# Three-layer EdgeConv graph network on one core: the next row's first edge by a product, and rows of A at a pitch of 512 elements

## The chip, the cores and the metric

The kernel runs on one core of one Trainium2 chip. The metric is the device time of one execution in microseconds. Three runs of the kernel before gave 522.43, 522.38 and 520.69 us, so its median is 522.38 us.

## What is computed

There are 2500 nodes with 256 features and 80,000 edges, sorted by destination. The reference normalizes x by rows, applies a ReLU, sends the result through three EdgeConv layers that average over each node's incoming edges, and multiplies all four feature matrices by a final weight.

```python
def _edge_conv(x, src, dst, W, b):
    xi = x[dst]
    xj = x[src]
    m = jnp.concatenate([xi, xj - xi], axis=-1) @ W + b
    s = jax.ops.segment_sum(m, dst, num_segments=N)
    cnt = jax.ops.segment_sum(jnp.ones((dst.shape[0],), m.dtype), dst, num_segments=N)
    return s / jnp.maximum(cnt, 1.0)[:, None]
...
h = jnp.maximum(_layernorm(x, axis=-1), 0.0)
for W, b in ((W0, b0), (W1, b1), (W2, b2)):
    h = jax.nn.relu(_edge_conv(h, src, dst, W, b))
    xs.append(h)
x = x + jnp.concatenate(xs, axis=-1) @ Wf + bf
```

## The kernel before

The kernel turns the sum over edges into a product with a matrix of counts: A[i, j] is how often node i is the source of an edge to node j. A layer is then the product of z = h times the lower half of the weight with A, plus a product of h with the difference of the weight's halves, weighted by the node's count. z is split into a high part zh and a low part zl, both in the 32-bit format fp32r, so each product with A is made twice.

The 2500 destination nodes are cut into 417 windows of 6, and the windows into five groups, four of 84 windows (504 columns of A) and one of 81 (486 columns). The part of A for one group is a tile `a` of 128 partitions by NT = 20 rows (of source nodes) by G = 504 columns (`new_a`, line 733). Two such tiles live in two pools, `apool0` and `apool1`, which take turns. A group's tile is built in the first layer (`build`, `counts`, `take_counts`: comparisons on VectorE, small products on TensorE, a copy by ScalarE), stored to DRAM (`finish`, line 788) and loaded again in the layers after (`load_a`, line 794), except for the two groups whose tiles are still held.

`layer` (line 802) makes one group of one layer: for each of the 20 rows and each of the two halves o it multiplies zh and zl with the row `a[:, i, :n]` (line 817), 80 products in all. Eight products with the weight `wt` follow or are mixed in (line 821), and ScalarE takes the result. Three layers of five groups make 1200 products with A. In the first layer they run through an order-keeping wrapper, so that the profile gives them the wrapper's line 280. In the layers after, they stand at line 817. `nodes_split` (line 692) makes the next z, with the bias row `brow` for the last tile of nodes, and `final` (line 715) the product with the final weight.

Before A can be built, the kernel must find where each window's edges begin. The destinations are laid out as 128 rows of 625 (`dst_i`). `find_first` (line 494) takes the first entry of each row as `first`, and the first entry of the row after it as `after`; that second one comes from a separate load, `next_i`, of 127 single numbers with a stride of a row (line 408). `find_rows` (line 499) compares both with the windows' limits `limr`, which gives `behind` and the selection `pick`. `pick_half` multiplies `pick` with the destinations, `count_half` counts on ScalarE, `search` makes the edges' offsets, and `get_edges` gathers them by GpSimd's indirect DMAs.

The order of work in this first part, the head, is written out by hand as a string of names (line 849) that `perform` runs through: each name issues its instructions on its engine, and each engine keeps that order. The names that matter here are `warm22` (22 products with a tile of zeros, made ahead of the next product that asks for it: `keep_warm`, `warmed`), `lim` and `io` (small constants), `dstr` (destinations to fp32r on ScalarE), `st0 rs0 sq0 sc0 N0` (statistics, square root on ScalarE, scales, and normalization of the first two tiles of x), `first`, `pick`, `pk00` and so on (`pick_half`), `sg` (`count_half`), `se` (`search`), `ge` (`get_edges`), `T`, `R` (transposes and their copies), `Z` (product with the layer's weight `wb`) and `F` (product with the final weight `wf`).

The loads at the start stand in the order of SP's queue: x tiles 0 and 1, `next_i`, x tiles 2 to 5, `wb`, x tiles 12 to 19, `wf`, `wt`, then three bias rows into `brow`. ScalarE's queue has the destinations and x tiles 6 to 11.

Tiles are laid out one after another in the order of their pools and names: `const`, `wpool` (weights), `hot` (comparisons), then `apool0` and `pre` or `apool1`. In the kernel before, `a` begins at byte 148,320 of a partition in `apool0` and at 188,640 in `apool1`. Both are 96 modulo 128. A row of A has 504 elements of 4 bytes, 2016 bytes, so that rows 0, 1, 2, 3 of four begin at 96, 64, 32 and 0 modulo 128, and so on around.

Of the kernel before, what the change touches and what calls it, by code (L numbers as in the profile page):

```python
# [8 lines left out]
F32 = mybir.dt.float32  # L9
I32 = mybir.dt.int32  # L10
AF = mybir.ActivationFunctionType
OP = mybir.AluOpType
# [4 lines left out]
def general(ctx: ExitStack, tc: tile.TileContext, x, src, dst, Ws, bs, Wf, bf, out):  # L17
# [12 lines left out]
    EB = J * P  # L30
    G = 512
    NG = NP // G
    TG = G // P
    KL = 5
    CELLS = NP * NP
    BIG = 4096.0
    assert E == NCH * P and NCH == NB * J and NP % G == 0 and NT % KL == 0 and EB < BIG
    assert CELLS + EB < 2 ** 24
# [84 lines left out]
    def count_block(b):  # L123
        row = ps_big.tile([P, 2, G], F32, name="big").rearrange("p a n -> p (a n)")
        for j in range(J):
# [73 lines left out]
    def group(l, g):  # L199
        hl, hn = h[l % 2], h[(l + 1) % 2]  # L200
        pa = ps_big.tile([P, 2, G], F32, name="big")
        if l == 0:
# [39 lines left out]
    for l in range(L):  # L242
        for g in range(NG):
            group(l, g)
# [21 lines left out]
F32R = mybir.dt.float32r  # L266
# [20 lines left out]
def run(it):  # L287
    for _ in it:
        pass
# [16 lines left out]
def chain(*its):  # L306
    for it in its:
        yield from it
# [3 lines left out]
def by_windows(ctx: ExitStack, tc: tile.TileContext, x, src, dst, Ws, bs, Wf, bf, out, missing):  # L312
    nc = tc.nc
    PE, DVE, ACT, POOL, SP = nc.tensor, nc.vector, nc.scalar, nc.gpsimd, nc.sync
    PEo, DVEo, POOLo, ACTo, SPo = (InOrder(tc, e) for e in (PE, DVE, POOL, ACT, SP))
    P = 128
    N, D = x.shape
    E = src.shape[0]
    NT = (N + P - 1) // P
    NP = NT * P  # L320
    LAST = N - (NT - 1) * P
    L = len(Ws)
# [13 lines left out]
    while sum(GWS) < NW:  # L336
        GWS.append(min(84, NW - sum(GWS)))
    G = max(GWS) * W
    NG = len(GWS)
    Q = NT // 2  # L340
    assert NT == 2 * Q
    PAD = 96
# [7 lines left out]
    const = ctx.enter_context(tc.tile_pool(name="const", bufs=1))  # L350
# [9 lines left out]
    def bank():  # L360
        return ps[-1].tile([P, 512], F32, name="bank")
# [8 lines left out]
    away = const.tile([P, WG, CAP], BF16, name="away")  # L370
    cnt = const.tile([P, NP], BF16, name="cnt")
    share = const.tile([P, NT], F32, name="share")
    brow = const.tile([P, L, D], F32, name="brow")
    bf_sb = const.tile([P, D], F32, name="bf_sb")
    ident = const.tile([P, P], F32, name="ident")
    ones = const.tile([P, 1], F32, name="ones")
    ones_b = const.tile([1, 1], BF16, name="ones_b")
    ident_b = const.tile([P, P], BF16, name="ident_b")
# [4 lines left out]
    nc_ = const.tile([P, W + 2], F32, name="nc_")  # L383
    deg_b = const.tile([P, WG, W], BF16, name="deg_b")
    lim = const.tile([P, WG], F32, name="lim")
    a_dram = [dram.tile([P, NT, G], F32, name=f"a_dram{g}") for g in range(NG)]

    apools = [ctx.enter_context(tc.tile_pool(name="apool0", bufs=1))]
    pre = ctx.enter_context(ExitStack())
    pp = pre.enter_context(tc.tile_pool(name="pre", bufs=1))  # L390
    pw = pre.enter_context(tc.tile_pool(name="prework", bufs=2))


    dst_rows = dst.rearrange("(p c) -> p c", p=P)
# [5 lines left out]
    def load_x(queue, a, b):  # L400
        queue.dma_start(acc[:, a:min(b, NT - 1), :], xr[:, a:min(b, NT - 1), :])
        if b == NT:
            queue.dma_start(acc[:LAST, NT - 1, :], x[(NT - 1) * P:N, :])

    chunks = [(0, 2), (2, 6), (6, 12), (12, NT)]
    load_x(SPo, *chunks[0])
    next_i = pp.tile([P, 1], I32, name="next_i")
    SPo.dma_start(next_i[:P - 1], dst_rows[1:P, 0:1])
    load_x(SPo, *chunks[1])
    load_x(ACTo, *chunks[2])  # L410
    ws = [None] * L
# [2 lines left out]
    def load_wb(l, queue=SP):  # L414
        ws[l] = wpool.tile([P, DC, D], F32, name="wt"), wpool.tile([P, DC, D], F32, name="wb", bufs=1)
        queue.dma_start(ws[l][1], Ws[l][D:2 * D, :].rearrange("(c p) d -> p c d", p=P))

    def load_wt(l, queue=SP):
        queue.dma_start(ws[l][0], Ws[l][0:D, :].rearrange("(c p) d -> p c d", p=P))
# [14 lines left out]
    row_i = pp.tile([P, MORE], I32, name="row_i")  # L434
    POOLo.iota(row_i, pattern=[[0, MORE]], base=-P, channel_multiplier=1)
    make_identity(nc, ident)
    im_i = pp.tile([P, NT * S], I32, name="im_i")
    POOL.iota(im_i, pattern=[[1, NT * S]], base=0, channel_multiplier=0)
    POOL.memset(brow, 0.0)
    nc_i = pp.tile([P, W + 2], I32, name="nc_i")  # L440
    POOL.iota(nc_i, pattern=[[-1, W + 2]], base=1, channel_multiplier=0)
    for l in range(L):
        SP.dma_start(brow[PAD:PAD + 1, l, :], bs[l].rearrange("(o d) -> o d", o=1))
    DVE.memset(ones, 1.0)
    DVE.memset(ones_b, 1.0)
    DVE.memset(cnt[:, NV:], 0.0)
# [12 lines left out]
    def warmed(to):  # L459
        for _ in range(cold[0]):  # L460
            PEo.matmul(to, idle[:, :P], idle, start=True, stop=True)
        cold[0] = 0
        return to
# [5 lines left out]
    first = pp.tile([P, 1], F32, name="first")  # L469
    after = pp.tile([P, 1], F32, name="after")  # L470
    behind = pp.tile([P, WG * P], F32, name="behind")
    pick = pp.tile([P, WG * P], F32R, name="pick")
# [14 lines left out]
    def limits():  # L487
        DVEo.tensor_copy(lim, lim_i)
        DVEo.tensor_copy(limr, limr_i)
        DVEo.tensor_scalar(unlim, lim, -1.0, 0.5, op0=OP.mult, op1=OP.add)  # L490
        DVEo.memset(after, float(2 ** 20))
        DVEo.tensor_copy(dst_r[:, :MORE], row_i)

    def find_first():
        DVEo.tensor_copy(first, dst_i[:, 0:1])
        DVEo.memset(first[0:1], -1.0)
        DVEo.tensor_copy(after[:P - 1], next_i[:P - 1])

    def find_rows():
        DVEo.tensor_scalar(behind, limr, after, None, op0=OP.is_gt)  # L500
        DVEo.scalar_tensor_tensor(pick, limr, first, behind, op0=OP.is_gt, op1=OP.subtract)

# [143 lines left out]
    turned, pz = {}, {}  # L646
# [45 lines left out]
    def nodes_split(l, t):  # L692
        pz = bank()
        for c in range(DC):
            PE.matmul(pz[:, :D], hT[:, c, t * P:(t + 1) * P], ws[l][1][:, c, :],  # L695
                      start=(c == 0), stop=(c == DC - 1))
        sc = share[:, t:t + 1]
        if t == NT - 1:
            zf = hot.tile([P, D], F32, name="zf")
            DVE.scalar_tensor_tensor(zf, pz[:, :D], sc, brow[:, l, :], op0=OP.mult, op1=OP.add)  # L700
            ACT.copy(zh[:, t, :], zf)
            DVE.tensor_sub(zl[:, t, :], zf, zh[:, t, :].bitcast(F32))
        else:
            ACT.activation(zh[:, t, :], pz[:, :D], AF.Copy, scale=sc)  # L704
            DVE.scalar_tensor_tensor(zl[:, t, :], pz[:, :D], sc, zh[:, t, :].bitcast(F32),  # L705
                                     op0=OP.mult, op1=OP.subtract)
# [22 lines left out]
    def touched(g):  # L729
        c0, n = group_of(g)  # L730
        return [t for t in range(NT) if (t + 1) * P > c0 and t * P < c0 + n]

    def new_a(g):
        return apools[g % 2].tile([P, NT, G], F32R, name="a")

    windows = [(g, s, min(BW, GWS[g] - s)) for g in range(NG) for s in range(0, GWS[g], BW)]
    ones_of = {}
# [47 lines left out]
    def finish(g, a):  # L785
        c0, n = group_of(g)
        POOLo.tensor_copy(a[PAD:PAD + 1, NT - 1, :n], cnt[PAD:PAD + 1, c0:c0 + n])
        SP.dma_start(a_dram[g][:, :, :n], a[:, :, :n].bitcast(F32))
        yield
# [12 lines left out]
    def layer(l, g, a, own, PE=PE, ACT=ACT):  # L802
# [29 lines left out]
    groups = [(0, 1), (1, 2), (2, 4), (4, 6), (6, 8), (8, Q)]  # L832
    a = new_a(0)
    acts = {
        "lim": limits, "first": find_first, "pick": find_rows,
        "dstr": lambda: ACTo.copy(dst_r[:, MORE:], dst_i),
        "pk": lambda i: pick_half(i // 10, i % 10), "sg": lambda i: count_half(i // 10, i % 10),
        "se": lambda i: search(*((0, 1), (1, WG))[i]), "ge": get_edges,
# [8 lines left out]
        "warm": keep_warm,  # L847
    }
    order = """
        warm22 lim io dstr st0 rs0 first sq0 sc0 N0 pick pk00 sg00 pk01 sg01 st1 T0 pk11 R0 st4 rs1 sq1 pk30 se0  # L850
        sg11 sc1 Z0 pk20 N1 st5 sg30 ge0 T1 st6 R1 rs3 F0 sg20 pk21 sq3 st7 pk10 H0 F1 rs4 st3 sq4 sc4 G0 st9
        sc3 L0 sg21 N6 pk31 ka0 kb0 Z1 N5 st8 N7 G1 T6 rs5 sg10 sg31 km0 T5 se1 kt0 R6 H1 st2 F6 sq5 sc5 k10 k20
        rs2 Z6 ge1 L1 T7 B0 R5 R7 Z5 B1 C0 B2 ka1 G6 H6 N9 H5 C1 T9 F7 E0 ge2 kb1 R9 sq2 km1 E1 kt1 C2 B3 k21 Z9
# [19 lines left out]
    def later_loads():  # L873
        load_wb(1, SPo)
        load_wt(1, SPo)
        load_wf(1, SPo)
        SPo.dma_start(bf_sb, bass.AP(tensor=bf.tensor, offset=bf.offset, ap=[[0, P], [1, D]]))
        yield
# [5 lines left out]
    extra = chain(degrees(0), finish(0, a), later_loads(), degrees(1))  # L884
    for g in range(NG):
        at = {}
        own = LATE
        if g + 1 < NG:
            a1 = new_a(g + 1)
# [20 lines left out]
        if g + 1 < NG:  # L910
            run(finish(g + 1, a1))
            held, a = a, a1
# [3 lines left out]
    for l in range(1, L):  # L916
        groups = list(range(NG))
        if l % 2:
            groups.reverse()

        last = touched(groups[0])
        for t in [t for t in range(NT) if t not in last] + last:
            nodes_split(l, t)
        if l + 1 < L:
            load_wb(l + 1)
            load_wt(l + 1)
        finished = set()
        for j, g in enumerate(groups):
            for t in touched(g):
                if t not in finished:  # L930
                    finished.add(t)
                    final(l, t)
                    if l == 1:
                        add_x(t)
            if j == NG - 1:
                load_wf(l + 1)
            run(layer(l, g, tiles[g], LATE))
            if j == 1 and l + 1 < L:
                DVEo.tensor_sub(ws[l + 1][0], ws[l + 1][0], ws[l + 1][1])
            if j + 2 < NG:  # L940
                del tiles[g]
                tiles[groups[j + 2]] = load_a(groups[j + 2])
# [41 lines left out]
```

## Time and profile before

| | |
|---|---|
| median of three runs | 522.38 us (520.69 to 522.43) |
| the profiled execution's own time | 522.35 us |
| its span, first to last instruction | 520.4 us |
| TensorE busy, share of the span | 512.0 us, 98% |
| VectorE, ScalarE, GpSimd busy | 213.8, 138.2 and 69.8 us |
| head, until the first product with A | 64.5 us |
| first layer's products and the building of A | 64.5 to 214 us |
| second and third layer, and the last products | 214 to 520.4 us |
| moved by DMA | 68.74 MB |

A line of the profile's groups names the line of the kernel, the engine, the operation, the tiles that it writes and reads, how often it was run, its total and mean time, and what the engine waited for just before. A product's own duration (some 390 ns for 504 columns) is longer than its share of TensorE's time, since products overlap: what one costs is the distance from its start to the start of the next.

### The profile page before, as it was taken

The numbers are of one execution on the slowest core, as the hardware profiler recorded it, in microseconds if no ns is written. First come the engines' busy times: TensorE is split into PE (matmuls) and PEld (weight loads), VectorE is DVE, ScalarE is ACT, GpSimd is POOL, SyncE is SP. The second block draws the span as 40 slices with busy tenths as digits, with TensorE's granted clock in tenths as the row PEclk, the third lists the DMA queues.
The fourth block names the chain that finished last, engine by engine and source line by source line (L and its number), as shares of the span: only waits on it lengthen the run. The fifth ranks groups of instructions, "written<-read, shape, count | busy, mean of one in ns | idle before, by whom it ended". The sixth has DMA issues, their size and how long they took to land.

```text
span 520.4 us, 6987 instructions
## 1 busy us (share of the span) xinstructions
PE 512.0 (98%) x2864; PEld 406.8 (78%) x2864; DVE 213.8 (41%) x455; ACT 138.2 (27%) x307; POOL 69.8 (13%) x102
## 2 busy tenths in 40 slices
PE   7999999999999999999999999999999999999996
PEld 3888878677777778788787878787887878787875
DVE  6899989888797950251101010102501010101033
ACT  5787567553633330340000000003400000000000
POOL 2591000000000000008133323200000000000000
PEclk9999999999999999999999999999999999999999
DMA  9110008840905319001556464100006363630023
GB/s 277 38 51 1 1 2 342 323 203 1 398 1 246 153 34 359 23 20 52 201 232 244 204 247 192 31 1 1 1 0 243 155 248 150 238 145 20 1 82 122
DMA packets 16351, 68.74 MB, mean 132 GB/s; under 512 B 1328, under 2 KB 14152, under 8 KB 15158
## 3 DMA queue, kind: packets, MB, share of 16 engines
q1 hardware_dynamic: 14038, 63.49, 31.2%
q0 software_dynamic: 1344, 3.61, 2.3%
q10 hardware_dynamic: 928, 1.11, 0.7%
q8 instruction: 24, 0.39, 0.3%
q14 instruction: 17, 0.14, 0.1%
HBM read 40.03 MB, written 28.18 MB: 131 GB/s over the span
## 4 chain that ended last, share of the span: by engine, by line
PE 96%; DVE 1%; DMA 1%; issue 0%; ACT 0%; SPq 0%
PE pa L817 35%; PE pa L280 21%; PE bank L718 10%; PE bank L280 9%; PE bank L695 7%; PE pa L821 6%; PE pz L280 6%; DMA next_i<-in_dst_dram 1%; PE turned L280 1%; DVE one_m L280 0%; DVE one_n L280 0%; ACT junk L280 0%; DVE pick L280 0%; DVE zl L280 0%; ACT hT L280 0%
## 5 line engine op out<-in xcount | busy, mean ns | idle before, releaser
L817 PE MATMUL pa<-a,zh 128*128 128x504 f32 (+1 forms) x400 | 157.6, 394 | 0.0
L817 PE MATMUL pa<-a,zl 128*128 128x504 f32 (+1 forms) x400 | 155.5, 389 | 0.0
L720 DVE SCALAR_TENSOR_TENSOR acc<-bank,share,acc 128x256 f32<-128x256 f32 x60 | 29.0, 484 | 214.8 <-PE bank L718 214.8
L817 PEld LDWEIGHTS pa<-a,zh 128*128 128x128 f32 x400 | 75.3, 188 | 15.6
L817 PEld LDWEIGHTS pa<-a,zl 128*128 128x128 f32 x400 | 75.2, 188 | 15.3
L280 PE MATMUL pa<-a,zh 128*128 128x504 f32 (+1 forms) x200 | 85.1, 426 | 0.0
L280 DVE TENSOR_TENSOR one_m<-iota_m,key_m 128x1024 bf16<-128x1024 bf16 (+1 forms) x105 | 71.9, 685 | 15.7 <-PE bank L280 15.4
L280 PE MATMUL pa<-a,zl 128*128 128x504 f32 (+1 forms) x200 | 77.8, 389 | 0.0
L824 ACT ACTIVATE hT<-pa 128x1008 f32<-128x1008 f32 (+1 forms) x10 | 10.0, 1005 | 240.2 <-PE pa L821 240.2
L280 ACT CAST a<-bank 128x480 fp32r<-128x480 f32 (+1 forms) x105 | 54.5, 561 | 66.7 <-PE bank L280 63.9
L280 DVE TENSOR_TENSOR one_n<-iota_n,key_n 128x960 bf16<-128x960 bf16 (+1 forms) x105 | 68.6, 653 | 0.0
L280 PEld LDWEIGHTS <-one_m 128*128 128x128 bf16 x834 | 45.6, 98 | 14.2 <-DVE one_m L280 7.5
L280 PE MATMUL bank<-one_n,one_m 128*128 128x120 bf16 x834 | 54.1, 217 | 0.3 <-DVE one_n L280 0.2
L718 PE MATMUL bank<-wf,hT 128*128 128x256 f32 x240 | 53.6, 379 | 0.0
L718 PEld LDWEIGHTS bank<-wf,hT 128*128 128x128 f32 x240 | 45.6, 190 | 9.9 <-issue 4.1
L280 PEld LDWEIGHTS pa<-a,zh 128*128 128x128 f32 x200 | 37.8, 189 | 9.1 <-issue 2.3
L280 PEld LDWEIGHTS pa<-a,zl 128*128 128x128 f32 x200 | 37.7, 189 | 8.2 <-issue 2.3
L705 DVE SCALAR_TENSOR_TENSOR zl<-bank,share,zh 128x256 fp32r<-128x256 f32 x38 | 18.4, 484 | 56.0 <-ACT zh L704 56.0
L821 PE MATMUL pa<-hT,wt 128*128 128x504 f32 (+1 forms) x80 | 35.2, 583 | 0.0
L695 PE MATMUL bank<-wb,hT 128*128 128x256 f32 x160 | 34.9, 379 | 0.0
L695 PEld LDWEIGHTS bank<-wb,hT 128*128 128x128 f32 x160 | 30.4, 190 | 4.9 <-issue 0.9
L821 PEld LDWEIGHTS pa<-hT,wt 128*128 128x128 f32 x80 | 15.2, 189 | 14.5 <-issue 13.8
(110 smaller groups left out, 339.2 us busy)
## 6 DMA issues: line engine op xcount, KB each, us to landing
a<-a_dram SPq DMA_DIRECT2D x5, 5040.0 KB, 15.8
a_dram<-a SPq DMA_DIRECT2D x4, 5040.0 KB, 15.4
a_dram<-a SPq DMA_DIRECT2D x1, 4860.0 KB, 17.1
a<-a_dram SPq DMA_DIRECT2D x1, 4860.0 KB, 15.7
zf<-in_x_dram POOLq DMA_DIRECT2D x19, 128.0 KB, 2.3
out_dram<-acc SPq DMA_DIRECT2D x19, 128.0 KB, 1.7
wf<-in_L_gnn_Wf_dram SPq DMA_DIRECT2D x4, 256.0 KB
acc<-in_x_dram SPq DMA_DIRECT2D x1, 896.0 KB, 8.4
```

What stands on the lines that cost most here:

```text
L280: return self.tc.keep_in_program_order(call(*args, **kwargs))
L695: PE.matmul(pz[:, :D], hT[:, c, t * P:(t + 1) * P], ws[l][1][:, c, :], start=(c == 0), stop=(c == DC - 1))
L705: DVE.scalar_tensor_tensor(zl[:, t, :], pz[:, :D], sc, zh[:, t, :].bitcast(F32), op0=OP.mult, op1=OP.subtract)
L718: PE.matmul(po[:, :D], hT[:, c, t * P:(t + 1) * P], wfs[l][:, c, :], start=(c == 0), stop=(c == DC - 1))
L720: DVE.scalar_tensor_tensor(acc[:, t, :], po[:, :D], share[:, t:t + 1], acc[:, t, :], op0=OP.mult, op1=OP.add)
L817: PE.matmul(pa[:, o, :n], z[:, i, o * P:(o + 1) * P], a[:, i, :n], start=(i == 0 and z is zh), stop=(z is zl and last[o] == (kind, i, o)))
L821: PE.matmul(pa[:, o, :n], ws[l][0][:, c, o * P:(o + 1) * P], hT[:, c, c0:c0 + n], start=False, stop=(last[o] == (kind, i, o)))
L824: ACT.activation(hT[:, :, c0:c0 + n], pa[:, :, :n], AF.Relu)
```

## The change

The load `next_i` is gone. `first` is multiplied by an identity matrix with one column more (`shift`, 128 by 129, whose first 128 columns serve as `ident` and whose last is zero): taken from its second column on, it moves each row's first edge to the row ahead. `find_rows` adds this product to `after`, which now holds 2^20 for the last row and zero elsewhere. In the written order `first` and the new `next` stand ahead of `dstr`, and the 22 warming products become 8 ahead of the new product and 12 ahead of `pk00`.

The rows of A stand GS = 512 elements apart in the tile (in DRAM still G = 504), of which at most 504 are used. `brow` keeps two bias rows instead of three, so the third layer's row is loaded later, into the place of the first. `ident` leaves the pool `const`, and an unused tile of 24 elements, `between`, ends that pool.

```diff
+    GS = 512
...
-    brow = const.tile([P, L, D], F32, name="brow")
+    brow = const.tile([P, 2, D], F32, name="brow")
     bf_sb = const.tile([P, D], F32, name="bf_sb")
-    ident = const.tile([P, P], F32, name="ident")
...
+    const.tile([P, 24], F32, name="between")
...
+    shift = pp.tile([P, P + 1], F32, name="shift")
+    ident = shift[:, :P]
...
     load_x(SPo, *chunks[0])
-    next_i = pp.tile([P, 1], I32, name="next_i")
-    SPo.dma_start(next_i[:P - 1], dst_rows[1:P, 0:1])
     load_x(SPo, *chunks[1])
...
+    POOL.memset(shift[:, P:], 0.0)
     POOL.memset(brow, 0.0)
...
-    for l in range(L):
-        SP.dma_start(brow[PAD:PAD + 1, l, :], bs[l].rearrange("(o d) -> o d", o=1))
+    def load_b(l, queue=SP):
+        queue.dma_start(brow[PAD:PAD + 1, l % 2, :], bs[l].rearrange("(o d) -> o d", o=1))
+
+    load_b(0)
+    load_b(1)
...
-        DVEo.memset(after, float(2 ** 20))
+        DVEo.tensor_scalar(after, row_i[:, 0:1], -1.0, float(2 ** 20), op0=OP.is_ge, op1=OP.mult)
...
         DVEo.memset(first[0:1], -1.0)
-        DVEo.tensor_copy(after[:P - 1], next_i[:P - 1])
+
+    ahead = []
+
+    def find_next():
+
+        ahead.append(warmed(bank()))
+        PEo.matmul(ahead[0][:, 0:1], shift[:, 1:], first, start=True, stop=True)
 
     def find_rows():
+        DVEo.tensor_add(after, ahead[0][:, 0:1], after)
         DVEo.tensor_scalar(behind, limr, after, None, op0=OP.is_gt)
...
-            DVE.scalar_tensor_tensor(zf, pz[:, :D], sc, brow[:, l, :], op0=OP.mult, op1=OP.add)
+            DVE.scalar_tensor_tensor(zf, pz[:, :D], sc, brow[:, l % 2, :], op0=OP.mult, op1=OP.add)
...
-        return apools[g % 2].tile([P, NT, G], F32R, name="a")
+        return apools[g % 2].tile([P, NT, GS], F32R, name="a")
...
-        "lim": limits, "first": find_first, "pick": find_rows,
+        "lim": limits, "first": find_first, "next": find_next, "pick": find_rows,
...
-        warm22 lim io dstr st0 rs0 first sq0 sc0 N0 pick pk00 sg00 pk01 sg01 st1 T0 pk11 R0 st4 rs1 sq1 pk30 se0
+        warm8 lim io first next dstr st0 rs0 sq0 sc0 warm12 N0 pick pk00 sg00 pk01 sg01 st1 T0 pk11 R0 st4 rs1 sq1 pk30 se0
...
         if l + 1 < L:
+            load_b(l + 1)
             load_wb(l + 1)
```

## The prediction

> **What bounds the kernel now.** First the page's totals and its chain that ended last: which engine fills the span, and which lines carry the chain.
>
> ```profile
> PE 512.0 (98%) x2864; PEld 406.8 (78%) x2864; DVE 213.8 (41%) x455; ACT 138.2 (27%) x307; POOL 69.8 (13%) x102
> PE 96%; DVE 1%; DMA 1%; issue 0%; ACT 0%; SPq 0%
> ```
>
> TensorE makes up 96% of the chain. The change can act in two ways: shorten the part that is not TensorE, or make TensorE's products follow each other faster. Second, the chain in order of time (start, length, what).
>
> ```profile
> 1.25 6.42 DMA next_i<-in_dst_dram
> 11.66 3.62 PE pz L280 x8
> 15.92 1.73 PE pz L280 x8
> ...
> 260.06 18.28 PE pa L817 x80
> 278.34 3.38 PE pa L821 x8
> ```
>
> The chain begins with 6.42 us of the load that the change removes. The first eight `pz` products take 3.62 us, later ones 1.73 us. And 80 products with A take 18.28 us, 228.5 ns each. Third, VectorE's timeline after that load.
>
> ```profile
> 7.70 0.15 DVE L280 CAST after<-next_i 127x1 f32<-127x1 int32 x1 [1.62 <-DMA next_i<-in_dst_dram]
> 7.77 0.15 DVE L280 RECIPROCAL rs<-rs 128x2 f32<-128x2 f32 x1
> 7.96 0.16 DVE L280 SCALAR_TENSOR_TENSOR off<-mv,rs 128x2 f32<-128x2 f32 x1
> 8.03 0.48 DVE L280 TENSOR_SCALAR behind<-limr,after 128x512 f32<-128x512 f32 x1
> 8.55 0.75 DVE L280 SCALAR_TENSOR_TENSOR pick<-limr,first,behind 128x512 fp32r<-128x512 f32 x1
> 9.46 0.43 DVE L280 BATCH_NORM_STATS2 st<-acc 128x6 f32<-128x256 f32 x1 [0.17 <-DMA acc<-in_x_dram]
> ```
>
> VectorE stands 1.62 us for `next_i`, and `sc0` (the reciprocal) is queued behind it. The last line matters as much: the next step, `st1`, waits for x tiles 2 to 5, so the load behind `next_i` on SP's queue is late next. Fourth, the busy time by stretches with the granted clock (PEclk).
>
> ```profile
> 8.50:11.80 3.30, 1.92 (x9) 1.26 (x10) 3.03 (x16) 2.68 (x10) 0.00 (x0) 1.00 1.11 337
> 11.90:15.20 3.30, 3.30 (x9) 2.59 (x9) 3.12 (x17) 1.89 (x7) 2.15 (x2) 0.50 0.52 149
> 15.30:18.70 3.40, 3.40 (x20) 3.08 (x20) 1.62 (x8) 2.74 (x10) 0.39 (x1) 1.00 0.14 39
> ```
>
> After a stretch with few products the clock was halved for one stretch, from 11.86 to 15.27 us: that is why the first `pz` products took 427 ns each instead of 216.
>
> **What the Trainium skill says.** "TensorE: Matmul & The Clock Gate", section "Part 1: The HAM clock gate", says that the clock falls to half after a window of some 3.4 us with little work, and that the windows run freely. The trace agrees (3.41 us at 0.50). The same page, "Back-to-back issue gap", gives N/2.4 + 2.5 ns between starts; for 504 columns an estimate of 212.5 ns. The 256-column fp32 products, which stream twice, agree (215.8 ns), but the products with A do not: 228.5 ns. "SBUF — State Buffer", section "Operand start alignment", says only that element alignment is legal and that nothing was timed, so it has no price for an alignment. "DMA: Bandwidth & Descriptors", section "Why a DMA increments its semaphore by 16 and not by 1", says that a DMA over 127 partitions lands on one engine; the trace agrees in that `next_i` took 6.42 us for half a kilobyte.
>
> **The alignment, step by step.** I took the starts of the 80 line-817 products of each 504-column group from the trace and averaged the distance to the next start by the row of A, leaving out the first two rows. Rows 0, 1, 2, 3 of four begin at 96, 64, 32, 0 modulo 128 bytes, and their distances are 229.27, 226.45, 229.75 and 228.86 ns, the same in every round of four. Their mean is 228.58. The row at 64 is the cheapest. For the 486-column group the same four are 221.47, 219.50, 219.62 and 221.64, mean 220.56; 64 is again lowest. In the new kernel the pool before `a` loses 1024 bytes (`brow`) and 512 (`ident`) and gains 96 (`between`), so `a` begins at 148,320 - 1440 = 146,880, which is 64 modulo 128. The second tile begins 20 x 2048 bytes later, 64 again, and a pitch of 2048 keeps all rows there. If each product then costs what row 1 costs now, 960 products x 2.13 ns = 2.05 us, and 240 x 1.06 ns = 0.25 us: **2.3 us**, all on TensorE, which sets the end in all three layers (no wait of TensorE over 0.6 us from 66 to 193 us). Both ends of this unknown: within row 1 the four positions run from 225.0 to 229.2 ns, so a uniform stream could settle at 225.0 (a gain of 4.1 us with the 486-column rows at 217.6) or at 229.2 (a loss under 1 us). I take the row's mean.
>
> **The head, step by step.** `first` moves ahead of `st0` on VectorE. Destinations land at 4.28 (ScalarE's wait), so `first` is done by 4.5, ahead of x's landing at 4.74: nothing. The eight warming products at half clock (427 ns) end at 1.54 + 3.42 = 4.96. The new product is not in the trace; its nearest rows, a 128-column weight load (0.19 to 0.30) and a short product (0.27 to 0.39), put it between 0.45 and 0.7 us, done by 5.7. The twelve more products end about 5.6 + 12 x 0.216 = 8.2. The statistics are unchanged, and ScalarE's root is done at 6.15; `sc0` without the wait ends at 6.54. The new addition costs 0.15 to 0.2 (`base<-base`, 0.15), then `behind` and `pick` as now, 8.03 to 9.30: done at 8.0 instead of 9.30, and `pk00` starts at 8.2 instead of 9.45, **1.29 us earlier**. `Z0` starts at 10.37, just after `wb` has landed (10.2 now, 0.41 earlier without the issue of `next_i`, 1.25 to 1.66).
>
> What is late next? With only 2.2 us of thin work before `Z0`, I expect the clock to stay full: `Z0` takes 1.73 and ends at 12.1. `T1` then waits for `N1`, which hangs on x tiles 2 to 5: 9.46 now, 9.05 then, so `N1` ends at 12.84 and `T1` starts near 12.95 instead of 15.32. `F0` follows at 13.4 instead of 15.76, so TensorE is 2.36 ahead. VectorE stood 1.74 us at 17.82 for ScalarE's root, which follows `T1`; its own work then ends 0.41 earlier than 16.08, so it goes on at 15.7, 2.1 ahead. From 44 to 50 us the chain runs over VectorE's comparisons (TensorE waits 0.34 and 0.30 there), so VectorE's **2.1 us** is what the head keeps. If x tiles 2 to 5 land much earlier, up to 3.0.
>
> **What costs nothing, and under what cover.** `after` as a comparison instead of a fill: 0.1 to 0.2 us on VectorE at 2.1, which is idle until 4.7. GpSimd's one-column fill (0.1) against a smaller `brow` fill (0.80 now for 768 elements, about 0.53 for 512): a gain nobody waits for. The bias row of layer 2 moves behind the stores on SP's queue, at 231 us, ahead of `wb` and `wt`: one issue, 0.43 us (1.28 for three now), for data used after 356 us. The `a` transfers change from runs of 40,320 bytes to 2016:
>
> ```profile
> a_dram<-a SPq DMA_DIRECT2D x4, 5040.0 KB, 15.4
> a_dram<-a SPq DMA_DIRECT2D x1, 4860.0 KB, 17.1
> a<-a_dram SPq DMA_DIRECT2D x1, 4860.0 KB, 15.7
> ```
>
> The 486-column group already goes in runs of 1944 bytes and takes 15.7 to 17.1 us, so at most 1.7 us more each. A load issued at 253.4 is used at 285.2, 16 us after it lands now: hidden. Without the cover it would be 1.7 us for each of nine. Weights and comparison tiles move by 1440 bytes too; their products stand at the price of N columns plus 2.5 to 3.5 ns already, so I take nothing, with 1 ns on some 1200 of them (1.2 us) as the bound upward.
>
> **The sum**, against the profiled execution's 522.35 us (span 520.4 and 1.95 around it; the median is 522.38): 522.35 - 2.1 - 2.3 = **518.0**.
>
> **Rivals.** (1) *The clock halves again.* If the window from 11.86 to 15.27 is still at half, `T1` takes 0.87 and three of `F0`'s products 0.43 each: `F0` ends at 16.35 instead of 17.49, a gain of 1.1, and 518.95. For: the windows run freely. Against: the thin stretch is a third shorter. (2) *Alignment buys nothing*, because the distances come from a rhythm over several rows that a uniform pitch merely re-times: 522.35 - 2.1 = 520.25. For: positions within one row differ by more than rows do. (3) *A uniform 225.0*: 522.35 - 2.1 - 4.1 = 516.1. (4) *Slower: a uniform stream sticks at its worst.* Single distances of 234 ns (504 columns) and 228 (486) recur; if all rows at one alignment meet that case each time, it costs 960 x 5.4 + 240 x 7.4 = 7.0 us, less 2.1: 527.3. It decides above 230.3 ns a product, where 1.75 ns x 1200 eats the head's gain. Against: the row at 64 shows no such value on average.
>
> **Chances.** Both gains 0.45; rival 1, 0.15; rival 2, 0.17 (with a lost head gain 0.21); rival 3, 0.07; rival 4, 0.12. Half a per cent (2.6 us, about what a measurement can tell from no change) is passed by the first, rivals 1 and 3, less 0.03 for a median of clock states: faster 0.64. Within: rival 2 and these, 0.24. Slower: 0.12. The range from 516.0 to 521.5 leaves out rival 4 and some of 3, and takes in rival 2 with its bound of 1.2 us upward.
>
> **What would show it.** No `next_i` in the chain; `pick` done near 8.0 and `F0` near 13.4; the clock at 1.00 from 8 to 15 us; the 80-product pieces of the chain at 18.1 us instead of 18.28, with all rows alike near 226.5; loads of `a` near 17 us and no wait on them. A stream over 230.3 ns, a wait on the new product, or VectorE's stretch from 44 to 50 us not moving would make it wrong.

## The result, and the profile after

The changed kernel takes 518.41 us (median of six runs, 517.92 to 518.61). The kernel before takes 522.38 us (six runs, the first three among them, 520.69 to 523.89). The ratio is 0.9925, with a 95% interval from 0.9906 to 0.9944. The profiled execution took 518.31 us, with a span of 516.4.

The totals and the chain that ended last, on the page of the changed kernel:

```profile
PE 509.2 (99%) x2864; PEld 405.9 (79%) x2864; DVE 213.9 (41%) x455; ACT 138.4 (27%) x307; POOL 70.1 (14%) x103
PE 96%; DMA 2%; DVE 0%; issue 0%; SPq 0%
```

The chain in order of time (start, length, what):

```profile
0.74 3.81 DMA dst_i<-in_dst_dram
...
5.08 8.54 DMA wf<-in_L_gnn_Wf_dram
13.67 1.99 PE pz L280 x8
...
257.02 18.15 PE pa L831 x80
...
473.31 17.68 PE pa L831 x80
```

`next_i` is gone, and the `wf` load has taken its place in the chain until 13.62 us. From 13.67 us on, TensorE carries the chain but for the very end; the pieces of VectorE's comparisons from 44 to 50 us are gone too. In the kernel before, this was one of them:

```profile
47.64 0.68 DVE one_m L280
```

The 80 products of a 504-column group take 18.15 us instead of 18.28, those of the 486-column group 17.68 instead of 17.65.

VectorE's timeline where the selection is made:

```profile
4.57 0.15 DVE L280 CAST first<-dst_i 128x1 f32<-128x1 int32 x1 [1.25 <-DMA dst_i<-in_dst_dram]
6.81 0.15 DVE L280 TENSOR_TENSOR after<-bank,after 128x1 f32<-128x1 f32 x1
...
7.52 0.75 DVE L280 SCALAR_TENSOR_TENSOR pick<-limr,first,behind 128x512 fp32r<-128x512 f32 x1
8.83 0.75 DVE L280 BATCH_NORM_STATS2 st<-acc 128x6 f32<-128x256 f32 x2 [0.56 <-DMA acc<-in_x_dram]
```

`pick` is done at 8.27 us instead of 9.30, and x tiles 2 to 5 have landed by 8.83 instead of 9.46. TensorE's timeline over the same stretch:

```profile
4.98 0.56 PE L280 MATMUL bank<-first,shift 128*128 128x1 f32 x2
5.40 3.34 PE L280 MATMUL bank<-idle 128*128 128x512 bf16 x12
8.42 0.62 PE L280 MATMUL bank<-dst_r,pick 128*128 128x314 f32 x2
...
10.72 1.99 PE L280 MATMUL pz<-wb,hT 128*128 128x256 f32 x8
...
13.67 1.13 PE L280 MATMUL pz<-wf,hT 128*128 128x256 f32 x4 [0.36 <-DMA wf<-in_L_gnn_Wf_dram]
```

The new product is out of the way by 5.4 us. The first eight `pz` products take 1.99 us instead of 3.62: the clock did not halve there, after it had once risen at 6.63 us. Last, the transfers of A with their time to landing:

```profile
a<-a_dram SPq DMA_DIRECT2D x5, 5040.0 KB, 17.3
a_dram<-a SPq DMA_DIRECT2D x4, 5040.0 KB, 17.2
```

They were 15.8 and 15.4 us. No wait of TensorE on a transfer of A appears from 66 us on, so the longer transfers stay hidden.

**Where the time went.** The first product with A started at 64.46 us and now starts at 61.68: 2.78 us. The first layer's end (the first `wb` product after it) came 149.51 us later and now comes 149.20 later: 0.31 us. The next two layers, to the last block of final products, took 284.19 and now take 283.22: 0.97 us. That is 4.06 us, against 522.35 - 518.31 = 4.04.

### The profile page after: what moved, and what is told of

Read it like the earlier page. It is cut to its first block, busy times and chain, and to the rows that moved or that the text cites. A ratio compares the mean times of both kernels' runs of the same rounds, so it can differ in the third digit from the quotient of the medians.

```text
span 516.4 us, 6986 instructions
## 1 busy us (share of the span) xinstructions
PE 509.2 (99%) x2864; PEld 405.9 (79%) x2864; DVE 213.9 (41%) x455; ACT 138.4 (27%) x307; POOL 70.1 (14%) x103
## 4 chain that ended last, share of the span: by engine, by line
PE 96%; DMA 2%; DVE 0%; issue 0%; SPq 0%
PE pa L831 35%; PE pa L280 21%; PE bank L732 10%; PE bank L280 10%; PE bank L709 7%; PE pz L280 7%; PE pa L835 6%; DMA wf<-in_L_gnn_Wf_dram 2%; DMA dst_i<-in_dst_dram 1%; PE turned L280 1%; DVE acc L734 0%; DVE first L280 0%; SPq L280 0%
## 5 line engine op out<-in xcount | busy, mean ns | idle before, releaser
L280 DVE TENSOR_TENSOR one_m<-iota_m,key_m 128x1024 bf16<-128x1024 bf16 (+1 forms) x105 | 72.4, 690 | 15.4 <-PE bank L280 15.2
## 6 DMA issues: line engine op xcount, KB each, us to landing
a<-a_dram SPq DMA_DIRECT2D x5, 5040.0 KB, 17.3
a_dram<-a SPq DMA_DIRECT2D x4, 5040.0 KB, 17.2
```

The costliest lines, as they stand in the source:

```text
L280: return self.tc.keep_in_program_order(call(*args, **kwargs))
```

## The experiments

Two theories were to be told apart for each half. For the rows: does the byte at which they begin set a product's price, or only that all of them are alike? For the head: is its gain the load that is gone, or the clock that no longer halves? The kernel before ran beside each batch: 521.15 us median (520.42 to 523.72, 22 runs) beside the first four experiments, 520.86 us (520.53 to 523.79, 40 runs) beside the next four, and 522.31 us (520.86 to 523.27, 11 runs) beside the last. Its times gather near 520.6 and near 522.4, which matters below; for the same reason the ratios, taken over all runs, differ a little from the quotients of the medians.

**The head alone** (`e1_head_only`): the changed kernel with its rows undone.

```diff
-        return apools[g % 2].tile([P, NT, GS], F32R, name="a")
+        return apools[g % 2].tile([P, NT, G], F32R, name="a")
-    const.tile([P, 24], F32, name="between")
+    const.tile([P, 32], F32, name="between")
```

> The change without its rows: A at a pitch of 504 elements, the first row at 96 modulo 128 as in the kernel before, and the product and the order of the change. If the two halves add, the head alone keeps what the traces show at the first product with A, about 2.5 us: near 519.9 us, and the distances by row go back to 229.3, 226.5, 229.8 and 228.9 ns (mean 228.6). If the gain came from the rows, it stands near 522.4 us.

It took 519.34 us (519.18 to 519.78), a ratio of 0.9956 (0.9939 to 0.9972). The first product with A starts at 61.52 us, and the rows are back at 229.27, 226.46, 229.69 and 228.85 ns. Two of its groups in the chain:

```profile
282.14 18.28 PE pa L831 x80
...
474.33 17.65 PE pa L831 x80
```

**The rows alone** (`e2_rows_only`): the kernel before with these edits.

```diff
+    GS = 512
-    brow = const.tile([P, L, D], F32, name="brow")
+    brow = const.tile([P, 2, D], F32, name="brow")
+    const.tile([P, 24], F32, name="between")
-        return apools[g % 2].tile([P, NT, G], F32R, name="a")
+        return apools[g % 2].tile([P, NT, GS], F32R, name="a")
```

The bias rows are loaded as in the change.

> The kernel before with only the rows: pitch 512, first row at 64 modulo 128 (brow two rows and the small pad to get there), the load of next_i kept. If the halves add: 1.6 us less, near 520.8 us, with 226.7 ns for every row of the 504-column groups and 221.1 ns for the 486-column ones. If the rows gain nothing on their own, 522.4 us.

It took 519.99 us (519.08 to 521.78), a ratio of 0.9970 (0.9954 to 0.9986). Two of its groups in the chain:

```profile
260.03 18.15 PE pa L822 x80
...
476.32 17.68 PE pa L822 x80
```

All 504-column rows stand at 226.7 ns, the 486-column rows at 221.1. From its first product with A to the last block of final products it takes 432.42 us, where the kernel before takes 433.71 and the changed kernel 432.42. So the rows are worth 1.3 us and the halves add: each alone is faster than the kernel before, each is slower than both together, and the two ratios multiplied give 0.9926, against 0.9925 for the change.

**Every row at 0, at 96 and at 32 modulo 128** (`e3_rows_at_0`, `e4_rows_at_96`, `e5_rows_at_32`): the changed kernel with an unused tile of n = 16, 8 or 24 elements ahead of A, so that only A and what lies after it move.

```diff
+    apools[0].tile([P, n], F32, name="pad")
     pre = ctx.enter_context(ExitStack())
```

> The changed kernel with an unused tile of 16 elements ahead of A alone, so that every row begins at 0 modulo 128. Theory 'the address counts': the rows at 0 cost what row 3 cost in the kernel before, 228.9 ns, 2.2 ns more than now on 960 products, so 2 us more, near 520.5 us. Rival 'only that all rows are alike counts': 226.7 ns and 518.4 us as now.

> The changed kernel with an unused tile of 8 elements ahead of A alone: every row begins at 96 modulo 128. Theory 'the address counts': 229.3 ns as row 0 in the kernel before, 2.5 us more, near 520.9 us. Rival 'only that all rows are alike counts': 226.7 ns and 518.4 us.

With both results known, the third was expected so:

> The changed kernel with an unused tile of 24 elements ahead of A alone: every row begins at 32 modulo 128. With rows at 64 and at 0 alike (226.7 and 227.0 ns) and rows at 96 dearer (228.9), the theory is now that only the start modulo 64 counts: 228.9 ns for 504 columns and 220.0 for 486, near 519.8 us. Rival 'each of the four starts has a price of its own, as the kernel before showed it': 229.8 ns, near 520.6 us.

They took, in this order, 518.49 us (ratio 0.9937, 0.9918 to 0.9956), 519.74 us (0.9962, 0.9946 to 0.9978) and 522.79 us (1.0028, 1.0018 to 1.0039). One 504-column group and the 486-column group in the chain, first with all rows at 0:

```profile
307.26 18.14 PE pa L832 x80
...
473.50 17.61 PE pa L832 x80
```

At 96:

```profile
308.03 18.31 PE pa L832 x80
...
475.30 17.60 PE pa L832 x80
```

At 32:

```profile
308.99 18.64 PE pa L832 x80
...
478.25 17.60 PE pa L832 x80
```

From start to start, averaged over the trace as in the prediction, a product costs:

| all rows begin at (modulo 128 bytes) | 504 columns | 486 columns | rows at that start in the kernel before, 504 columns |
|---|---|---|---|
| 64 (the change) | 226.67 ns | 221.1 ns | 226.45 ns |
| 0 | 227.0 ns | 221.1 ns | 228.86 ns |
| 96 | 228.9 ns | 220.0 ns | 229.27 ns |
| 32 | 233.3 ns | 220.0 ns | 229.75 ns |

Both sides of the first question fall in part. Being alike is not enough: at 32 the kernel is slower than the one before. But the price of a start is not what the mixed rows show for it either: at 504 columns, 0 is 1.9 ns cheaper alone than in the mixture, 32 is 3.6 ns dearer. The guess that only the start modulo 64 counts holds for 0 and 64 and fails for 32 and 96. It would hold for 486 columns, where the order is the other way round (220.0 ns at 32 and 96, 221.1 at 0 and 64).

**The load kept, the clock kept** (`e6_load_kept_warm`): the kernel before with one number changed.

```diff
-        warm22 lim io
+        warm27 lim io
```

> The kernel before with 27 warming products instead of 22 and nothing else: next_i is still loaded, but TensorE has work until about the time when pick is done. Theory 'a good part of the head's gain is the clock that no longer halves': the first eight pz products take 1.7 to 2.0 us instead of 3.6, and the upper half of the times of the kernel before (over 522 us) disappears: 520.5 us. Rival 'it is the load': as the kernel before, 520.4 to 523.7 us with the median near 521.2 to 522.4.

It took 521.08 us (520.41 to 521.62), a ratio of 0.9997 (0.9988 to 1.0007). TensorE's timeline:

```profile
1.54 8.91 PE L280 MATMUL bank<-idle 128*128 128x512 bf16 x27 [1.54 <-DVE idle L451]
10.10 0.64 PE L280 MATMUL bank<-dst_r,pick 128*128 128x314 f32 x2
...
12.43 1.99 PE L280 MATMUL pz<-wb,hT 128*128 128x256 f32 x8
```

The first `pz` products take 1.99 us, and no run stands over 522 us (12 of the 40 of the kernel before do): as the clock theory said. But the 27 products ran late, since the clock rose only at 7.48 us in this execution (5.03 in the profile before), and held the first selected product until 10.10 us. What the clock gave, the later start took back: the median is 0.6 us above the expectation and no lower than that of the kernel before.

**The load gone, the second warming gone** (`e7_no_second_warming`): the changed kernel with this edit.

```diff
-        sc0 warm12 N0 pick
+        sc0 N0 pick
```

> The changed kernel without the 12 warming products ahead of pk00. TensorE is then idle from about 5.5 to 8 us. Theory 'clock': it halves for a stretch of 3.4 us in most executions, the median is 1 to 2 us above the changed kernel's (519.4 to 520.4 us), and the times spread again by over 1.5 us. Rival 'it is the load': 518.4 us, or 0.2 us less, since pk00 need not wait for the last warming products.

It took 519.69 us (518.60 to 520.47), a ratio of 0.9968 (0.9957 to 0.9979). TensorE's timeline:

```profile
8.07 0.86 PE L280 MATMUL bank<-dst_r,pick 128*128 128x314 f32 x2 [2.72 <-DVE pick L280]
...
10.51 3.27 PE L280 MATMUL pz<-wb,hT 128*128 128x256 f32 x8
```

The selected product starts 0.35 us earlier than in the changed kernel, and still the eight `pz` products take 3.27 us: TensorE was at half clock there, until 13.1 us. The first product with A starts at 62.93 us, 1.25 us later. So the twelve warming products are worth 1.3 us in the median (taken on two occasions) and the even times (0.7 us from lowest to highest with them, 1.9 without). The head's gain is thus neither the load alone nor the clock alone.

**Two edits to go further** (`e8_wf_early_last_group_at_32`), the second of which then alone (`e9_last_group_at_32`). The labels say 32: the edit moves the rows by 32 bytes, to 96 modulo 128.

```diff
-    load_x(SPo, *chunks[3])
     load_wf(0, SPo)
+    load_x(SPo, *chunks[3])
...
-        return apools[g % 2].tile([P, NT, GS], F32R, name="a")
+        a = apools[g % 2].tile([P, NT, GS], F32R, name="a")
+        return a[:, :, 8:] if g == NG - 1 else a
```

> The changed kernel with two edits that the runs so far point to: the first wf loaded ahead of x tiles 12 to 19 (TensorE waited 0.36 to 0.59 us for it at the first F), and the 486-column group's rows begun 8 elements later, at 96 modulo 128, where they cost 220.0 ns instead of 221.1. The second is worth 240 x 1.1 ns = 0.26 us; the first up to 0.4 us, if VectorE does not become late for tiles 12 to 19, which land later. Together 517.8 us; if VectorE becomes late, 518.2 us or more.

> The changed kernel with only the second edit of the run before: the 486-column group's rows begin 8 elements later, at 96 modulo 128. 240 products x 1.1 ns: 0.26 us less than the changed kernel, 518.15 us, and 17.60 us instead of 17.69 for that group's 80 products. If it stands at 518.4 us or more, the start of these rows is worth nothing that can be measured, and the early load of wf did not cost what the run before seemed to show.

The first took 518.57 us (518.46 to 518.67; ratio 0.9949, 0.9933 to 0.9964), the second 517.93 us (517.85 to 518.70; ratio 0.9928, 0.9910 to 0.9945). The 486-column group fell to 17.60 us in both, so that edit works, for 0.08 us each time; in both traces the stretch from the first product with A to the last block of final products is 432.15 us instead of 432.42, the 0.26 us that was expected. The median of the second lies 0.5 us below the changed kernel's, but on another occasion and with runs on both sides of it, so the times alone don't tell it from 518.41.

The early `wf` let the first `F` start at 12.80 us instead of 13.67, but the first product with A starts at 62.10 us, later than the changed kernel's 61.68. Two places of the chain show where the lead went:

```profile
3.09 9.50 DMA acc<-in_x_dram
...
23.39 3.32 POOL acc L280 x2
...
41.67 0.68 DVE one_m L280
```

At 26.7 us TensorE waited for tiles of x that GpSimd normalizes, at the end of a chain that begins with the load of x tiles 12 to 19, and between 41 and 48 us it waited for VectorE's comparisons again. That is the other outcome that the expectation named. But the later x tiles can't be shown to be its cause: without the early `wf`, in the second run's profile, GpSimd's step stands in the chain at the same time, VectorE's comparisons do so until 48 us, and the first product with A starts at 62.25 us.

```profile
23.35 3.31 POOL acc L280 x2
...
46.60 0.68 DVE one_m L280
```

So in these two profiles a start of `F` that is 0.9 us earlier bought almost nothing, because GpSimd and VectorE were not earlier. Why all times of the first lie at 518.46 us or above, while four of the six of the second lie at 518.00 or below, stays open: the profile of the second is of its slowest run.

## Why the prediction came true, step by step

The sum was 522.35 - 2.1 - 2.3 = 518.0, and 518.31 was measured. The two mechanisms acted as forecast, but both terms were off, in opposite directions: the head gave 2.8 us, the rows 1.3. That the sum comes within 0.3 us is in part luck.

**The selection.** Done at 8.27 us, predicted 8.0. That `next_i` took 6.42 us does not by itself show that it lay on one DMA engine, since it stood behind x tiles 0 and 1 in its queue. The destinations and the first x tiles landed 0.3 us later than in the profile before, and the chain behind them shifted with them. `pk00` started at 8.42 (predicted 8.2), 0.15 us after `pick` as before. The clock rose only at 6.63 us, so that the twelve warming products took 3.34 us instead of 2.6 and were just out of the way.

**The clock.** The step "I expect the clock to stay full" held in the profile after, and the `pz` products took their 1.99 us. The Trainium skill's page "TensorE: Matmul & The Clock Gate", section "Part 1: The HAM clock gate", says that the windows run freely; the traces here agree, since full clock begins at 5.03, 6.63, 4.38 and 7.48 us in four profiled executions. The section speaks of an idle window before the clock falls; in the kernel before, TensorE was busy for 1.92 of the 3.30 us from 8.50 to 11.80 us, and the clock fell all the same. What the prediction left out is how much the clock governs the kernel before. Its times gather near 520.6 and 522.4 us, and the mean granted clock of each execution goes with the group: of the 73 runs beside the experiments, all 24 above 522.2 us have a clock between 0.991 and 0.997, and 46 of the 49 below 522 us have 0.998 or more (the other three 0.997). One halved window of 3.41 us lowers the mean over 520 us by 0.003; a half clock at the very end, as in the changed kernel's profile from 515.2 us on, counts too. So the upper group is, in all likelihood, the executions with a halved window; where it lies is seen only in the profiles (of the kernel before, 522.35 us, and of the rows alone, 521.23 us), and there it is at the first `pz` products. By this reading the head's 2.8 us are about 1.3 to 1.5 us from the selection's earlier start (519.34 us against 520.6, or against 520.86, the median of the lower group beside it) and 1.5 to 1.8 us from the clock. The measured ratio depends on which group fills the median: from 520.6 the change gains 2.2 us, from 522.4 it gains 4.0. Rival 1, the clock that halves again, did not happen. In e7's profile the first `pz` products ran at half clock too, but there the clock had not risen before.

**What is late next.** I named x tiles 2 to 5 and expected them at 9.05; they came by 8.83, and `T1` started at 12.70 instead of the predicted 12.95. The wait that did decide was not named: `wf`, in the chain until 13.62, so that `F0` started at 13.67 instead of 13.4. From `wf`'s landing on, the chain is TensorE's own: it is 2.09 us ahead at `F0`, and 0.64 us more come from the two waits for comparisons between 44 and 50 us (0.34 and 0.30), which are gone. That makes 2.73 of the 2.78 us at the first product with A. VectorE was ahead enough for it: it went on at 15.30 us (predicted 15.7), 2.5 us ahead instead of 2.1. So the term "VectorE's 2.1 us is what the head keeps" was too small for this execution, in which VectorE no longer held TensorE at all.

It is not so in every execution. The profiles of the rows at 96, at 32 and of the last run have the same head, but in them VectorE's comparisons stand in the chain until some 48 us and the first product with A starts at 62.35, 62.04 and 62.25 us, 2.1 to 2.4 us ahead of the kernel before: there the term was right. In those three, and in all other profiles with VectorE in the chain, two normalizations that GpSimd starts between 22 and 26 us take 3.3 us by the profile. In the three profiles without it (the change, the head alone, the rows at 0) they take 2.4 to 2.6:

```profile
23.21 2.38 POOL L280 TENSOR_SCALAR acc<-acc,rs,off 128x256 f32<-128x256 f32 x2
```

The gathers that GpSimd issues after them then start earlier, and VectorE waits for its last edges 0.5 to 0.7 us instead of 1.2 to 1.5. What makes GpSimd's step short or long is not shown. So 0.4 to 0.7 us of the head's 2.8 seem to be a matter of the execution.

**The rows.** The step "if each product then costs what row 1 costs now" came true to 0.2 ns for 504 columns (226.67 against 226.45). For 486 columns it failed: 221.1 ns instead of 219.5, a loss of 0.06 us a group where a gain of 0.08 was reckoned. And the runs at 0, 96 and 32 show that the reading was luckier than it was sound: by the same reading 0 would have cost 228.9 and 32 229.8, and they cost 227.0 and 233.3. In a mixture, it seems, a distance belongs to a row and its neighbours together. The first layer gave 0.31 us where 320 x 2.13 + 80 x 1.06 ns = 0.77 us was in the sum. There the products with A come 4 to 12 at a time between others, and eight of them take 1.88 us instead of 1.89. The next two layers gave 0.97 us of 1.53: their average fell by 1.9 instead of 2.1 ns, the first two rows of a group, left out of the averages, gained less, and the 486-column groups lost.

**The rivals.** Rival 2 (alignment buys nothing) is refuted by e2, rival 3 (225.0 everywhere) by the trace. Rival 4, a uniform stream at its worst, exists, but at another byte: rows at 32 cost 233.3 ns, and e5 is slower than the kernel before by 0.28%, although it has the head of the change (its first product with A starts at 62.04 us).

**What costs nothing.** The loads of A took 17.3 us instead of 15.8 and the stores 17.2 instead of 15.4, about the predicted 1.7 more, and stay hidden. The moved weights kept their 215.8 ns a product. The bias row loaded later appears in no wait.

What stays open: why the start of a row has a price at all, and why its order turns round between 504 and 486 columns. The runs give the prices, not the mechanism. Every uniform start was tried at a pitch of 2048 bytes, so a part played by the pitch itself is not excluded.

## What to carry to other kernels

When a wait at the start of a kernel is taken away, look at two things beside it: the load that is next in line, and whether TensorE now has enough work until its first real product to keep its clock; here each half was worth over 1 us of the head's 2.8. Where hundreds of long fp32r products stream one tile, measure the starts of its rows (here four, 32 bytes apart) with a small unused tile ahead of it, since a mixture of starts does not show what one start costs alone: from the first product with A on, 432.42 us at the best start became 436.91 at the worst. And an earlier first product is not an earlier end: follow the lead to where the long work begins, since by the traces GpSimd and VectorE took back all that an early `wf` gave.

## What was not expected of the hardware

The distance between fp32r products of 504 columns runs from 226.7 to 233.3 ns with the start of the moving rows, while fp32 products of 256 columns kept 215.8 ns when their weights moved by 1440 bytes. With 486 columns the order reverses: 220.0 ns at 32 and 96, 221.1 at 0 and 64. Eight warming products at half clock, 3.4 us of work, followed by a pause of 2.7 us, were not enough to raise the clock in e7's profile: full clock began only at 13.1 us, in the second half of the first real products. The same two normalizations on GpSimd take 2.4 to 2.6 us in three of eleven profiles and 3.3 us in the others.
